# A written-out order of four graph layers: rooms granted by "can every older graph still finish" in place of fixed reserves

## Chip, cores, metric

One core of a Trainium2 chip runs the whole program. The metric is device time in microseconds (us), lower is better. The kernel is launched once; everything it computes is in float32.

## What is computed

32 independent graphs, each with 512 nodes of 256 features `x` and a dense 512 x 512 adjacency `adj`. Every graph goes through four layers, one after the other, and each layer ends in a layer norm over the 256 features:

```python
# layer 0: aggregate with self loop, two dense layers (256 -> 512 -> 256)
x = LN(x + relu(((1 + eps) * x + adj @ x) @ W1 + b1) @ W2 + b2)
# layer 1: dense 256 -> 256, aggregate, leaky relu
x = LN(x + prelu(adj @ (x @ W.T + b), alpha))
# layer 2: norm, aggregate, two dense layers added, relu
h = LN(x) * gamma + beta
x = LN(x + x + relu((adj @ h) @ W_rel + b_rel + h @ W_root))
# layer 3: aggregate, dense 256 -> 1024, RMS norm, silu, dense 1024 -> 256
h = silu(RMS((eps * x + adj @ x) @ W1 + b1) * w)
x = LN(x + h @ W2 + b2)
```

Inside one graph nearly everything hangs on the step before it. Between graphs nothing does.

## The kernel before, in words

**The work of one graph.** All matrix products use a seven-product scheme (`seven`, L651) on half-size blocks: products m1 to m7 go to three PSUM banks that are opened one after the other, and between the products ScalarE or VectorE takes sums out of the banks. A product of `aggregate` (L767) is two matmuls with 256 columns. VectorE makes the sums and differences of blocks that the scheme needs, ScalarE most of the norms' totals, GpSimd the powers of -1/2, SyncE issues all DMAs.

**Buffers.** Three pools (L525 to L527) hold everything that comes and goes: 8 PSUM banks (`banks`), 36 SBUF rooms of 1024 floats per partition (`rooms`; half a room can be given), and 11 small ones (`smalls`). A graph's inputs take three rooms (`load_x` one, `Adjacency` two), and `FLIGHT = 5` (L499) lets at most five graphs hold buffers at once.

**The order.** The kernel does not leave the order to the program text. `do` and `move` (L279, L308) only record operations (`Op`), each with its graph, its possible engines, assumed durations and the operations that must come first. After all 32 graphs are recorded, `best` (L348) runs `order` (L354) once for each tuple of `RULES` and issues the operations in the order of the best one. This takes place when the program is built and costs the chip nothing. What reaches the chip is a fixed order for each engine's queue, and a fixed buffer for each operand.

`order` plays the program through. It gives every operation a `rank`: `graph * period + need`, where `need` (L324) is twice (`pace`) the TensorE work of its graph that lies ahead of it, minus what stands between; the last three graphs (`LATE`) lie only `last` apart. One graph's ranks run over about 142 units, `period` is 42 (the order of the kernel before comes from the tuple 42, 2, 10), so between three and four graphs are interleaved. At each step it takes, among the operations that can start at the earliest moment on an engine, the one of lowest rank. An operation that no TensorE work of its graph waits for (the last norm, the output) has a `need` of about 1000 and so comes last.

An operation that opens a buffer can be taken only if `rooms_free` (L380) allows it. There the change works. Before it, each pool has fixed reserves, `spare`, by the age of the graph (0 for the oldest graph that is not finished, 1 for the next, and so on): a bank is given to the oldest graph if one is free and to a younger one if two are free (0, 1, 1); a room needs 0, 2, 4, 4 further free rooms at ages 0, 1, 2, 3 and up; a small one 0, 2, 4.

```python
                    n += pool.spare[min(op.graph - oldest, len(pool.spare) - 1)]
                    if n >= len(whole):
                        return None
```

The instructions issued for the graphs are the same under any order: the same matmuls, vector, scalar and DMA operations, except that a few copies may go to another engine, and short filler writes (`pause`, L1197) are put in where VectorE has to wait for GpSimd.

Of the kernel before, what the change touches and what calls it, by code (L numbers as in the profile page):

```python
# [14 lines left out]
P = 128  # L15
# [52 lines left out]
ISSUE, ADVANCE, AFTER, LANES = dict(sync=0.45, within=0.66, gpsimd=1.5), 1.5, 0.8, 8  # L68


def wire_time(kbytes):
    return kbytes / 385
# [19 lines left out]

RULES = [(42, 2, 10, 0.5), (42, 2, 16, 0.5)]


class Pool:

    def __init__(self, tiles, grain, spare, psum):
        self.tiles, self.grain, self.spare, self.psum = tiles, grain, spare, psum
        self.clear()

    def clear(self):
# [30 lines left out]
class Room:  # L137
# [2 lines left out]

    def __init__(self, pool, whole=True):
        self.pool, self.whole = pool, whole
        self.uses = 0
        self.clear()

# [75 lines left out]
class Plan:  # L221
# [102 lines left out]
    def needs(self, pace, near):  # L324
# [20 lines left out]
            for op, t, b in zip(self.ops, need, between)  # L345
        ]

    def best(self):  # L348


        rule = min(RULES, key=lambda rule: self.order(*rule)[0])
        return self.order(*rule)[1]

    def order(self, period, pace, last, near):  # L354

        final = max(op.graph for op in self.ops) - LATE
        rank = [
            (min(op.graph, final) * period + max(op.graph - final, 0) * last + need, i)
            for i, (op, need) in enumerate(zip(self.ops, self.needs(pace, near)))
        ]  # L360
        behind = [op.behind for op in self.ops]
        ready = [dict.fromkeys(op.ways, 0.0) for op in self.ops]
        left = {}
        for op in self.ops:
            left[op.graph] = left.get(op.graph, 0) + 1
            for r in op.rooms:
                r.clear()
                r.pool.clear()
        free = dict.fromkeys(("tensor", "vector", "scalar", "gpsimd", "sync"), 0.0)
        oldest, wire, lanes = 0, 0.0, [0.0] * LANES  # L370
        port = dict.fromkeys(free, 0.0)
        powers = {i for i, op in enumerate(self.ops) if op.port and "gpsimd" in op.ways}
        can_start = {i for i, n in enumerate(behind) if not n}
        done = []
        while can_start:
            while oldest in left and not left[oldest]:
                oldest += 1
            room_at = {}

            def rooms_free(op):  # L380

                first = [r for r in op.rooms if r.index is None]
                if not first:
                    return 0.0
                if op.graph - oldest >= self.flight:
                    return None
                at, taken = 0.0, {}
                for r in first:
                    pool = r.pool
                    if pool not in room_at:  # L390
                        room_at[pool] = pool.free()
                    whole, halves = room_at[pool]
                    k = taken.get((pool, False), 0)
                    if not r.whole and k < len(halves):
                        taken[pool, False] = k + 1
                        at = max(at, halves[k][0])
                        continue
                    n = taken.get((pool, True), 0)
                    taken[pool, True] = n + 1
                    n += pool.spare[min(op.graph - oldest, len(pool.spare) - 1)]  # L400
                    if n >= len(whole):
                        return None
                    at = max(at, whole[n][0])
                return at

            best = {}
            for i in can_start:
                op = self.ops[i]
                wait = rooms_free(op)
                if wait is None:  # L410
                    continue
                if op.kbytes and "sync" in op.ways:
                    wait = max(wait, lanes[0])
                at = {
                    e: max(free[e], wait, ready[i][e], port[e] if op.port else 0.0) for e in op.ways
                }
                way = min(
                    at, key=lambda e: at[e] + sum(op.ways[e][0]) + YIELD * (op.yields and e == "vector")
                )
                best.setdefault(way, []).append((at[way], rank[i], i))  # L420
            if not best:
                return 1e12, None
            t, engine = min((min(c)[0], e) for e, c in best.items())
            soon = t + (1e-6 if engine == "tensor" else SOON)
            _, t, i = min((r, s, i) for s, r, i in best[engine] if s <= soon)
            op = self.ops[i]
            op.start, op.way = t, engine
            busy, tail = op.ways[engine][0]
            free_before, free[engine] = free[engine], t + busy
            end = t + busy + tail  # L430
            if engine == "vector":
                idle = t - max(free_before, ready[i][engine])
                op.pause = idle if op.port and t == port[engine] else 0.0
                if op.port:
                    port["gpsimd"] = end
                if any(n in powers for n, _ in op.then):
                    port["vector"] = t + busy + PORT
            if op.kbytes:
                wire = max(wire, t + ADVANCE) + wire_time(op.kbytes)
                end = wire + op.late + AFTER  # L440
                if engine == "sync":
                    lanes = [*lanes[1:], end]
            for r in op.rooms:
                if r.index is None:
                    r.pool.take(r)
                r.left -= 1
                r.until = max(r.until, end + 0.1)
            left[op.graph] -= 1
            for n, result in op.then:
                behind[n] -= 1  # L450
                for e in ready[n]:
                    if e != engine or e != "tensor" and result:
                        ready[n][e] = max(ready[n][e], end + HAND[e])
                if not behind[n]:
                    can_start.add(n)
            can_start.remove(i)
            done.append(op)
        return max(op.start for op in done), done


@with_exitstack
def tile_gnn_stack(ctx: ExitStack, tc: tile.TileContext, a: dict, out: bass.AP):
# [26 lines left out]
    B, N, D = a["x"].shape  # L489
    NC = N // P  # L490
# [8 lines left out]
    FLIGHT, ROOMS, SMALL = 5, 36, 11  # L499

    const = ctx.enter_context(tc.tile_pool(name="const", bufs=1))
    work = ctx.enter_context(tc.tile_pool(name="work", bufs=1))
    psum = ctx.enter_context(tc.tile_pool(name="psum", bufs=1, space=bass.MemoryType.PSUM))
# [12 lines left out]

        return plan.graph in (0, B - 1)

    def pool(kind, name, n, size, grain, spare):
        return Pool(  # L520
            [kind.tile([P, size], F32, tag=f"{name}{i}", name=f"{name}{i}") for i in range(n)],
            grain, spare, kind is psum,
        )

    banks = pool(psum, "ps", 8, N, N, (0, 1, 1))  # L525
    rooms = pool(work, "room", ROOMS, NC * D, P, (0, 2, 4, 4))
    smalls = pool(work, "few", SMALL, 64, 4, (0, 2, 4))  # L527


    def vector(method, n, *args, **kw):  # L530
# [51 lines left out]
    def room(*shape):  # L582
        return Part(Room(rooms)).shaped(*shape)
# [16 lines left out]
    class Wide:  # L600


        def __init__(self, n):
            self.n = n
            self.rooms = [room(2, N) for _ in range(n // 2)]
# [630 lines left out]
```

## Time and profile before

| what | value |
|---|---|
| median of 3 runs | 2318.81 us (2318.75 to 2318.9) |
| span of the profiled execution, first to last instruction | 2317.5 us |
| instructions | 41158, of them 14002 matmul records |
| VectorE, ScalarE, GpSimd busy | 2120.0 us (91%), 1642.6 us (71%), 256.9 us (11%) |
| DMA | 122.83 MB, mean 53 GB/s |
| granted TensorE clock | 0.999 |

The profiled execution's span lies 1.3 us under the median of the runs, which also hold what lies around the span. Nearly all records stand on one line, L298, because every operation is issued by one helper; so groups are told apart by the names of their tiles: `ps` is a bank, `room` a room, `few` a small one, `A` and `L_gnn_W` are weights. A float32 matmul stands in the trace as two records.

Besides the profile's own views, the kernel's recorded operations can be laid beside the trace: every engine runs its instructions in the order in which they were issued, and the counts agree exactly (6989 matmuls at two records and 24 transposes at one make 14002; 5343 vector operations, 161 on GpSimd, 1005 DMAs). This tells to which graph a record belongs, and which buffers are held when. Read so, graph 0 has matmuls from 9.2 to 205.1 us and is done at 261.6 us; graph 3 starts at 42.7 us, graph 4 at 96.9; graph 10 has matmuls from 636.7 to 909.0 us; graph 31, the last, from 2157.6 to 2308.6 us.

### The profile page before, as it was taken

The numbers are of one execution on the slowest core, as the hardware profiler recorded it, in microseconds if no ns is written. First come the engines' busy times: TensorE is split into PE (matmuls) and PEld (weight loads), VectorE is DVE, ScalarE is ACT, GpSimd is POOL, SyncE is SP. The second block draws the span as 40 slices with busy tenths as digits, with TensorE's granted clock in tenths as the row PEclk, the third lists the DMA queues.
The fourth block names the chain that finished last, engine by engine and source line by source line (L and its number), as shares of the span: only waits on it lengthen the run. The fifth ranks groups of instructions, "written<-read, shape, count | busy, mean of one in ns | idle before, by whom it ended". The sixth has DMA issues, their size and how long they took to land.

```text
span 2317.5 us, 41158 instructions
## 1 busy us (share of the span) xinstructions
PE 2295.5 (99%) x14002; PEld 2089.9 (90%) x14002; DVE 2120.0 (91%) x5428; ACT 1642.6 (71%) x4444; POOL 256.9 (11%) x167
## 2 busy tenths in 40 slices
PE   9999999999999999999999999999999999999998
PEld 7889899999999999999999999999999999998988
DVE  8989999999899999999999999989999899989897
ACT  4676677776776776777767776767677677676776
POOL 0000001101101101011011111010110101101110
PEclk9999999999999999999999999999999999999999
DMA  7001222112221122211222211222112222201101
GB/s 241 21 18 19 62 58 60 24 55 62 58 60 28 54 59 65 55 43 41 56 65 57 60 25 56 61 58 59 38 46 58 65 55 52 78 13 24 55 15 42
DMA packets 223746, 122.83 MB, mean 53 GB/s; under 512 B 142896, under 2 KB 194352, under 8 KB 223536
## 3 DMA queue, kind: packets, MB, share of 16 engines
q1 hardware_dynamic: 223536, 120.20, 19.1%
q8 instruction: 111, 1.82, 0.3%
q14 instruction: 99, 0.81, 0.1%
HBM read 78.92 MB, written 24.97 MB: 45 GB/s over the span
## 4 chain that ended last, share of the span: by engine, by line
PE 89%; DVE 7%; ACT 2%; DMA 1%; issue 1%; SPq 0%; POOL 0%; ACTq 0%; DVEq 0%
PE ps L298 89%; DVE room L298 6%; ACT room L298 1%; ACT scrap L298 1%; DVE few L298 1%; DMA room<-in_x_dram 1%; DMA L_gnn_W<-in_L_gnn_W_dram 0%; DMA room<-in_adj_dram 0%; DMA L_gnn_b<-in_L_gnn_b_dram 0%; DMA diagonal<-room 0%; SPq L316 0%; ACT L298 0%; DVE A L298 0%; DVE L_gnn_W_root L298 0%; POOL few L298 0%
## 5 line engine op out<-in xcount | busy, mean ns | idle before, releaser
L298 PE MATMUL ps<-room,room 128*128 128x256 f32 x3584 | 930.9, 381 | 5.7 <-DVE room L298 3.2
L298 DVE TENSOR_TENSOR room<-room,room 128x512 f32<-128x512 f32 (+1 forms) x1360 | 773.0, 590 | 5.4 <-ACT room L298 2.8
L298 DVE TENSOR_TENSOR room<-ps,room 128x256 f32<-128x256 f32 (+1 forms) x1344 | 605.6, 469 | 143.7 <-PE ps L298 136.4
L298 PEld LDWEIGHTS ps<-room,room 128*128 128x128 f32 x3584 | 617.3, 191 | 70.3 <-DVE room L298 7.1
L298 PE MATMUL ps<-L_gnn_W,room 128*128 128x128 f32 (+1 forms) x3584 | 544.3, 290 | 1.9 <-DVE room L298 1.0
L298 PEld LDWEIGHTS ps<-L_gnn_W,room 128*128 128x128 f32 x3584 | 505.6, 191 | 33.7 <-ACT room L298 1.9
L298 PEld LDWEIGHTS ps<-A,room 128*128 128x128 f32 x3072 | 460.5, 191 | 47.3 <-DVE room L298 14.1
L298 PE MATMUL ps<-A,room 128*128 128x128 f32 x3072 | 486.9, 276 | 0.9 <-DVE room L298 0.7
L298 POOL TENSOR_TENSOR few<-few,mhalf 128x4 f32<-128x4 f32 (+2 forms) x161 | 256.2, 1598 | 2054.5 <-DVE few L298 1883.1
L298 ACT ACTIVATE room<-room,few 128x256 f32<-128x256 f32 x627 | 335.0, 596 | 159.9 <-DVE few L298 159.7
L298 PE MATMUL ps<-room,L_gnn_W 128*128 128x256 f32 x1536 | 416.4, 380 | 0.6 <-DVE room L298 0.5
L298 ACT ACTIVATE room<-ps,L_gnn_b_c 128x256 f32<-128x256 f32 x768 | 311.0, 476 | 122.3 <-PE ps L298 117.9
L298 DVE TENSOR_TENSOR room<-room 128x256 f32<-128x256 f32 (+1 forms) x640 | 308.7, 492 | 13.9 <-ACT room L298 8.2
L298 PE MATMUL ps<-room,A 128*128 128x256 f32 x1152 | 320.0, 380 | 1.1 <-ACT room L298 0.8
L298 ACT ACTIVATE room<-room 128x1024 f32<-128x1024 f32 (+2 forms) x260 | 240.8, 939 | 87.3 <-DVE room L298 84.4
L298 PEld LDWEIGHTS ps<-room,L_gnn_W 128*128 128x128 f32 x1536 | 274.5, 191 | 30.1 <-DVE room L298 1.9
L298 ACT ACTIVATE room<-ps 128x256 f32<-128x256 f32 (+1 forms) x513 | 180.1, 373 | 153.3 <-PE ps L298 153.1
L298 ACT ACTIVATE scrap<-room,few 128x256 f32<-128x256 f32 x504 | 250.7, 499 | 39.0 <-DVE few L298 38.3
L298 ACT ACTIVATE scrap<-room 128x256 f32<-128x256 f32 x504 | 206.7, 411 | 88.3 <-DVE room L298 79.8
L298 PEld LDWEIGHTS ps<-room,A 128*128 128x128 f32 x1152 | 202.8, 191 | 22.8 <-ACT room L298 2.0
L298 ACT ACTIVATE room<-room,L_gnn_rms_weight_c 128x512 f32<-128x512 f32 x256 | 173.2, 712 | 13.1 <-DVE room L298 11.0
L298 DVE TENSOR_TENSOR room<-room,loop 128x256 f32<-128x256 f32 x256 | 101.1, 411 | 2.9 <-DMA diagonal<-room 1.8
(57 smaller groups left out, 1110.6 us busy)
## 6 DMA issues: line engine op xcount, KB each, us to landing
room<-in_adj_dram SPq DMA_DIRECT2D x128, 256.0 KB, 5.0
room<-in_x_dram SPq DMA_DIRECT2D x31, 512.0 KB, 5.9
out_dram<-room SPq DMA_DIRECT2D x31, 512.0 KB, 3.2
room<-room SPq DMA_DIRECT2D x480, 32.0 KB, 2.0
diagonal<-room SPq DMA_DIRECT2D x62, 128.0 KB, 1.8
room<-in_adj_dram SPq DMA_DIRECT2D x124, 64.0 KB, 1.9
room<-diagonal SPq DMA_DIRECT2D x62, 128.0 KB, 2.2
room<-line SPq DMA_DIRECT2D x30, 256.0 KB, 3.3
```

The costliest lines, as they stand in the source:

```text
L298: getattr(getattr(self.nc, engine), method)(to, *(put(x) for x in args), **kw)
```

## The change

Three things, all inside the ordering; the recorded operations are not touched.

- `peaks` gives for each operation, by pool, the most buffers that its graph will hold at once from there on. `safe` walks over the graphs in flight from the oldest: each must be able to get what it still needs (its peak, plus one except for banks, less what it holds) out of what is free and what the graphs before it give back. What is left over is what a younger graph may take. `spare` is gone.
- An operation of a graph that is not the oldest, on another engine than TensorE, which would open a buffer, is passed over while its rank is more than `AHEAD` = 70 above that of the first TensorE operation (by rank) not yet placed. Operations with a `need` of `LAST` = 500 or more are exempt.
- `RULES`, tuples of (period, pace, last, near), has (42, 2, 10), (44, 2, 12) and (46, 2, 10) in place of (42, 2, 10) and (42, 2, 16).

```diff
-RULES = [(42, 2, 10, 0.5), (42, 2, 16, 0.5)]
+RULES = [(42, 2, 10, 0.5), (44, 2, 12, 0.5), (46, 2, 10, 0.5)]
+AHEAD, LAST = 70.0, 500.0
...
+    def peaks(self):
+        first, last = {}, {}
+        for i, op in enumerate(self.ops):
+            for r in op.rooms:
+                first.setdefault(r, i)
+                last[r] = i
+        use, held = [], {}
+        for i, op in enumerate(self.ops):
+            for r in op.rooms:
+                if first[r] == i:
+                    k = r.pool, op.graph
+                    held[k] = held.get(k, 0) + r.size
+            use.append({r.pool: held[r.pool, op.graph] for r in op.rooms})
+            for r in op.rooms:
+                if last[r] == i:
+                    held[r.pool, op.graph] -= r.size
+        most, peaks = {}, [None] * len(self.ops)
+        for i in range(len(self.ops) - 1, -1, -1):
+            g = self.ops[i].graph
+            now = dict(most.get(g, {}))
+            for pool, n in use[i].items():
+                now[pool] = max(now.get(pool, 0), n)
+            most[g] = peaks[i] = now
+        return peaks
...
+            def safe(pool, free):
+                most, slack, older = [free], 1e9, 0.0
+                for g in range(oldest, oldest + self.flight):
+                    if left.get(g):
+                        need = peaks[mine[g][reached.get(g, 0)]].get(pool, 0) + (not pool.psum)
+                        has = held.get((pool, g), 0)
+                        slack = min(slack, free + older - max(need - has, 0))
+                        older += has
+                        most.append(slack)
+                    else:
+                        most.append(most[-1])
+                return most
...
-                    n += pool.spare[min(op.graph - oldest, len(pool.spare) - 1)]
-                    if n >= len(whole):
+                    if n >= min(len(whole), most[max(op.graph - oldest, 0)]):
                         return None
...
+            while ahead < len(tensor) and finished[tensor[ahead][1]]:
+                ahead += 1
+            front = tensor[ahead][0] + AHEAD if ahead < len(tensor) else 1e9
...
+                early = op.graph > oldest and front < rank[i][0] and need[i] < LAST
+                if early and "tensor" not in op.ways and any(r.index is None for r in op.rooms):
+                    continue
...
-    banks = pool(psum, "ps", 8, N, N, (0, 1, 1))
-    rooms = pool(work, "room", ROOMS, NC * D, P, (0, 2, 4, 4))
-    smalls = pool(work, "few", SMALL, 64, 4, (0, 2, 4))
+    banks = pool(psum, "ps", 8, N, N)
+    rooms = pool(work, "room", ROOMS, NC * D, P)
+    smalls = pool(work, "few", SMALL, 64, 4)
```

The rest keeps the books: what each graph holds, how far it has come (`reached`), and which operations are placed (`finished`).

More of the change, by code (lines that the diff above doesn't have):

```diff
@@ L90, with __init__ @@
 LATE = 3
-RULES = [(42, 2, 10, 0.5), (42, 2, 16, 0.5)]
+RULES = [(42, 2, 10, 0.5), (44, 2, 12, 0.5), (46, 2, 10, 0.5)]
+AHEAD, LAST = 70.0, 500.0
 class Pool:
-    def __init__(self, tiles, grain, spare, psum):
-        self.tiles, self.grain, self.spare, self.psum = tiles, grain, spare, psum
+    def __init__(self, tiles, grain, psum):
+        self.tiles, self.grain, self.psum = tiles, grain, psum
         self.clear()
@@ L142, in __init__ @@
         self.pool, self.whole = pool, whole
+        self.size = 1.0 if whole else 0.5
         self.uses = 0
@@ L356, in order @@
         final = max(op.graph for op in self.ops) - LATE
+        need = self.needs(pace, near)
         rank = [
-            (min(op.graph, final) * period + max(op.graph - final, 0) * last + need, i)
-            for i, (op, need) in enumerate(zip(self.ops, self.needs(pace, near)))
+            (min(op.graph, final) * period + max(op.graph - final, 0) * last + n, i)
+            for i, (op, n) in enumerate(zip(self.ops, need))
         ]
+        tensor = sorted(r for r, op in zip(rank, self.ops) if "tensor" in op.ways)
         behind = [op.behind for op in self.ops]
@@ L369, in order @@
         free = dict.fromkeys(("tensor", "vector", "scalar", "gpsimd", "sync"), 0.0)
-        oldest, wire, lanes = 0, 0.0, [0.0] * LANES
+        oldest, ahead, wire, lanes = 0, 0, 0.0, [0.0] * LANES
+        peaks, held, mine, reached = self.peaks(), {}, {}, {}
+        for i, op in enumerate(self.ops):
+            mine.setdefault(op.graph, []).append(i)
+        finished = [False] * len(self.ops)
         port = dict.fromkeys(free, 0.0)
@@ L390, in rooms_free @@
                     if pool not in room_at:
-                        room_at[pool] = pool.free()
-                    whole, halves = room_at[pool]
+                        whole, halves = pool.free()
+                        room_at[pool] = whole, halves, safe(pool, len(whole))
+                    whole, halves, most = room_at[pool]
                     k = taken.get((pool, False), 0)
@@ L443, in order @@
             for r in op.rooms:
+                k = r.pool, op.graph
                 if r.index is None:
                     r.pool.take(r)
+                    held[k] = held.get(k, 0) + r.size
                 r.left -= 1
                 r.until = max(r.until, end + 0.1)
+                if not r.left:
+                    held[k] -= r.size
             left[op.graph] -= 1
@@ L457, in order @@
             done.append(op)
+            finished[i] = True
+            n, my = reached.get(op.graph, 0), mine[op.graph]
+            while n < len(my) - 1 and finished[my[n]]:
+                n += 1
+            reached[op.graph] = n
         return max(op.start for op in done), done
@@ L517, in alone, with pool @@
         return plan.graph in (0, B - 1)
-    def pool(kind, name, n, size, grain, spare):
+    def pool(kind, name, n, size, grain):
         return Pool(
             [kind.tile([P, size], F32, tag=f"{name}{i}", name=f"{name}{i}") for i in range(n)],
-            grain, spare, kind is psum,
+            grain, kind is psum,
         )
-    banks = pool(psum, "ps", 8, N, N, (0, 1, 1))
-    rooms = pool(work, "room", ROOMS, NC * D, P, (0, 2, 4, 4))
-    smalls = pool(work, "few", SMALL, 64, 4, (0, 2, 4))
+    banks = pool(psum, "ps", 8, N, N)
+    rooms = pool(work, "room", ROOMS, NC * D, P)
+    smalls = pool(work, "few", SMALL, 64, 4)
     def vector(method, n, *args, **kw):
```

## The prediction

> **What bounds the kernel now.** I read the page's busy times first, then a table of windows, then the groups by shape, then single matmul runs in the timeline, and last the waits of TensorE, by stretches.
>
> ```profile
> PE 2295.5 (99%) x14002; PEld 2089.9 (90%) x14002; DVE 2120.0 (91%) x5428; ACT 1642.6 (71%) x4444; POOL 256.9 (11%) x167
> ```
>
> ```profile
> core 0: us, PE busy (x) PEld busy (x) DVE busy (x) ACT busy (x) POOL busy (x), PEclk, DMA share, GB/s
> 0.00:20.00 20.00, 15.40 (x62) 12.78 (x63) 14.82 (x47) 5.48 (x12) 0.70 (x6) 1.00 0.87 281
> 20.00:120.00 100.00, 96.53 (x537) 83.56 (x537) 96.71 (x266) 62.37 (x175) 6.31 (x5) 1.00 0.33 98
> 120.00:300.00 180.00, 177.41 (x1084) 160.57 (x1083) 164.71 (x422) 124.07 (x328) 17.16 (x12) 1.00 0.13 31
> 300.00:1900.00 1600.00, 1600.00 (x9775) 1461.28 (x9774) 1467.59 (x3727) 1157.32 (x3146) 185.18 (x112) 1.00 0.20 54
> 1900.00:2100.00 200.00, 198.42 (x1198) 180.22 (x1198) 183.42 (x484) 140.91 (x397) 20.09 (x14) 1.00 0.17 45
> 2100.00:2300.00 200.00, 199.27 (x1282) 183.47 (x1282) 186.39 (x460) 139.83 (x353) 24.04 (x15) 1.00 0.09 26
> 2300.00:2318.00 18.00, 8.44 (x74) 8.06 (x72) 6.41 (x28) 12.60 (x40) 3.38 (x4) 0.82 0.30 117
> ```
>
> TensorE (PE) is never idle from 300 to 1900 us; what it loses, it loses in the first 300 us and in the last 400. But "busy" alone can hide a slower stream, so I ask how fast matmuls follow each other when nothing holds them:
>
> ```profile
> 2272.38 1.03 PE L298 MATMUL ps<-room,A 128*128 128x256 f32 x4
> ...
> 2301.76 4.63 PE L298 MATMUL ps<-A,room 128*128 128x128 f32 x40
> ```
>
> ```profile
> L298 PE MATMUL ps<-room,room 128*128 128x256 f32 x3584 | 930.9, 381 | 5.7 <-DVE room L298 3.2 <-DMA room<-in_x_dram 2.5
> ...
> L298 PE MATMUL ps<-A,room 128*128 128x128 f32 x3072 | 486.9, 276 | 0.9 <-DVE room L298 0.7
> ```
>
> Forty 128-column records take 4.63 us, of which the last is 0.276 long: 39 steps of 0.1116 us. Four 256-column records take 1.03, the last 0.381: 3 steps of 0.2163. By the groups there are 7192 records of the first kind (3072 + 3072 + 512 + 512 + 16 + 8) and 6810 of the second (3584 + 1536 + 1152 + 512 + 18 + 8): 802.6 + 1473.0 = about 2276 us. The first matmul starts at 1.2 us and the last at 2308.7, so 2307.5 us hold 2276 of full-rate work and about 32 us of lost time (35 with the mean steps, 0.1112 and 0.2163, of undisturbed neighbours). Summed over the starts of neighbouring matmuls with those means, the 35 lie so: 5.5 before 20 us, 10.7 from 20 to 200, 1.5 to 300, 10 spread over 300 to 1900 in gaps of about 0.1 us, 7.5 after 1900. Behind the last matmul stand 8.8 us of norm and output of graph 31.
>
> Who is late in the head and in the middle, by the waits of TensorE and its weight loads:
>
> ```profile
> PE ps L298 <- DVE room L298: 4.3, 9, 1.5
> PE ps L298 <- DMA room<-in_x_dram: 2.3, 1, 2.3
> PE ps L298 <- ACT room L298: 1.5, 3, 0.7
> ...
> PE ps L298 <- DMA L_gnn_ln_beta_c<-in_L_gnn_ln_beta_dram: 1.1, 1, 1.1
> ```
>
> ```profile
> PEld ps L298 <- DVE room L298: 11.4, 44, 0.3
> PEld ps L298 <- issue: 4.3, 23, 0.3
> ```
>
> The first four are from 0 to 320 us, the last two from 320 to 1900. In the head a result of VectorE ends most waits, and VectorE is 97% busy from 20 to 120 us: there graph 0 is alone at the front, its steps hang on each other, and younger graphs only fill. In the middle no wait exceeds 0.3 us.
>
> **What the Trainium skill says.** "Perfetto Trace Analysis", section "Identifying the Most-Contended Engine", warns that matmul busy share is no measure of headroom and recommends that of LDWEIGHTS; this trace agrees that the 99% needs a second look: the step of 0.1116 us between records of 0.276 us gives it, and the 90% of the weight loads is reached at full rate. The same page, "Optimization Strategy", says that a gap repeating on the engine that should be saturated can mean that there isn't enough SBUF or PSUM for the next tile; from 300 to 1900 us no such gap is here, so more freedom with rooms and banks has nothing to cure there. The page's "Optimizing Tensor Performance" wants independent groups to rotate through PSUM banks so that an evacuation overlaps the next group's matmuls; how many banks a younger graph may rotate through is what the change regulates.
>
> **The change part by part.** The instructions stay, so the floor of 2276 us stays, and so do 1.2 us before, 8.8 behind, and nearly all of the 5.5 before 20 us (the first loads, 2.3 and 1.1 us, stand in the waits; the rest is ahead of any choice between graphs). What the change can win is at most 10.7 + 1.5 + 7.5 = 20 us in head and tail; the 10 us of the middle are too fine for it.
>
> *Rooms and banks in the middle.* I took the order of the kernel before, operation for operation, and applied the new rule's formula at each opening of a buffer: how often would it have said no? From 300 to 1900 us: never, in any pool. Where was the old reserve tight? Over the whole run 265 of 1033 bank openings and 145 of 1469 room openings stood at the old limit. So in the middle the new rule only loosens, on an engine without a gap. The loosening is free but worth 0 us; half of all matmuls there already had their operands 5 us ahead of their start, a quarter less than 2.3. Price between -1 and +2 us, since another order shifts the 0.1 us gaps; I take 0.
>
> *Banks in the head and tail.* Here the rule tightens. An older graph that still has products ahead reserves three banks even while it holds none. Of the bank openings of before, 22 would be refused between 0 and 300 us, 27 between 1900 and 2300. A refused opening moves a fill product of a younger graph (four records, 4 x 0.2163 = 0.87 us of TensorE) to later. If another product is at hand it costs nothing; if none, up to one of the visible waits on VectorE or ScalarE, 5.8 us in 12 waits from 0 to 320 us, 0.48 each. At most 49 x 0.48 = 24 us; below nothing at the other end: the oldest graph, which sets the head's pace, finds a bank at once, and could recover part of those 5.8 us. I take +2 for stalls and -3 for the earlier front: -1.
>
> *Rooms in the head.* Five openings between 113 and 127 us (graphs 1 and 3) would be refused; some minus, some plus, 0.
>
> *Held back.* With period 42, the order of before breaks the new limit of 70 just six times: the openings of the loads of graph 3 (issued at 28.9, 31.0, 33.7 us) and graph 4 (38.1, 41.8, 42.6). No VectorE or ScalarE operation breaks it, so VectorE's load of the head is not relieved. The six wait until the front reaches rank 46 and 88, which before it does at about 50 and 103 us. A load lands in 5 to 6 us. Graph 3 has 0.9 us of matmuls between 40 and 50 us and next to none until 90, graph 4 has 0.9 between 90 and 100 and then none until 200. So at most 1.8 us of fill are lost; in turn SyncE's queue and the DMA engines are freed from 29 to 43 us, where weights of layers 1 and 3 and the restored diagonals go through the same queue: at most the 0.5 + 0.7 us lost at 30.6 and 37.8 us come back. I take +0.5. In the middle a new graph's loads start when the graph five before it is done, at front ranks that allow them at once or some 10 us later, well ahead of use: 0.
>
> *RULES.* The tuple chosen before, (42, 2, 10), stays on offer; two others are added and one goes. A wider period means less interleaving. `best` takes another one only if it plans a shorter end, and what it can plan shorter is head and tail. The last graphs then fit into each other better: of the 7.5 us lost from 1900 on I take 2, between 0 and 4.
>
> Sum: 0 - 1 + 0 + 0.5 - 2 = -2.5 us. On the profiled execution 2317.5 - 2.5 = 2315.0; the median stands 1.3 above the span: 2316.3 us.
>
> **The rivals.** 0.2% of 2318.81 is 4.6 us, about what separates a change from no change here.
>
> 1. *About the same* (chance 0.42): the sum above, with its bounds from -4.6 to +4.6. For it: the middle never refuses. Time 2316.3.
> 2. *Clearly faster* (0.30): the reserve for the oldest graph and the better tail halve what is lost after 20 us outside the middle: (10.7 + 1.5 + 7.5) / 2 = 9.9, less the 1.8 us of lost fill: -8, 2311 us. For it: 72 of the openings by the youngest graphs alone stood at the old bank limit, so the old fill pressed on the old graphs. Against: VectorE is 97% full in the head and gets no relief.
> 3. *Slower* (0.28): three banks lie reserved for an old graph that is in its norm and can't use them, so five are left for all others; TensorE runs dry in the head, and with four graphs abreast also in the tail. Each of the 49 refused openings costs 0.25 us on average: +12 us, 2331. It decides from 4.6 / 49 = 0.09 us each. If the order in the middle also shifts so that the reserve bites there, this grows by some 0.3 us for each of about 22 graphs: +7. Against: such refusals are rare in the old order.
> 4. *The change does nothing* (within rival 1): the order comes out nearly as before, the time within 1 us.
>
> **How the numbers follow.** The likeliest is 1, so 2316.3. The range takes in rival 2 with half again its gain and rival 3 up to nearly its price: 2307 to 2329. The likeliest case's own range is 2314.2 to 2323.4. Chances: faster by over 0.2% 0.30, within 0.42, slower 0.28.
>
> **What would show it.** After the change, PE busy from 300 to 1900 us must stay at 1600 of 1600 (else rival 3 reaches the middle). The loads of graphs 3 and 4 must come after 45 and 85 us. The idle of PE from 20 to 300 us, 6.1 us by the windows, and from 1900 to 2300, 2.3 us, must change by little; if they halve it is rival 2, if waits on banks' evacuation (a PE wait on VectorE or ScalarE rooms) grow there it is rival 3. The matmul count must be 14002 and the tail behind the last matmul about 8.8 us. I am wrong if the middle loses or if the span's end moves by more than the head and the tail can give.

## The result, and the profile after

The changed kernel takes 2326.37 us (median of 5 runs, 2325.61 to 2328.35), the kernel before 2318.9 (2318.75 to 2319.18). The ratio is 1.0031, 95% interval 1.0019 to 1.0042: slower by 0.3%, about 7.5 us. The profiled execution has a span of 2323.8 us against 2317.5. Its matmul count is the same, 14002, and of the three tuples the plan took (42, 2, 10) again, so the edit of `RULES` did nothing. In the plan itself the two orders end alike, with the last operation at 2285.8 us in both: what was lost lies where the chip departs from the plan.

The same windows as those of the kernel before (first and last left out; columns: length, then busy time and records of PE, its weight loads, VectorE, ScalarE, GpSimd, then clock, DMA share, GB/s):

```profile
20.00:120.00 100.00, 95.49 (x525) 82.33 (x524) 94.63 (x262) 62.96 (x179) 6.32 (x5) 1.00 0.34 98
120.00:300.00 180.00, 178.67 (x1104) 162.99 (x1103) 171.20 (x437) 127.25 (x336) 18.12 (x13) 1.00 0.16 42
300.00:1900.00 1600.00, 1595.92 (x9740) 1460.59 (x9739) 1476.26 (x3700) 1136.87 (x3126) 166.95 (x111) 1.00 0.20 52
1900.00:2100.00 200.00, 198.90 (x1200) 181.46 (x1199) 181.30 (x466) 140.76 (x389) 18.64 (x13) 1.00 0.17 43
2100.00:2300.00 200.00, 197.36 (x1246) 179.93 (x1245) 183.16 (x457) 138.51 (x356) 23.19 (x14) 1.00 0.09 26
```

From 300 to 1900 us PE was busy for 1600 of 1600 us; now it is 1595.92. That was the first sign named in the prediction as one that would prove it wrong. The waits of PE and of its weight loads from 320 to 1900 us (total, times, longest):

```profile
PE ps L303 <- DVE room L303: 2.9, 11, 0.3
```

```profile
PEld ps L303 <- DVE room L303: 12.7, 23, 0.7
PEld ps L303 <- issue: 4.2, 22, 0.2
```

Before, PE had no wait at all in this stretch and its weight loads 44 on VectorE of at most 0.3 us. Now there are 23 of up to 0.7 us, about one for each graph that finishes in these 1580 us: a bubble that comes back with every graph.

Lost time, summed over the starts of neighbouring matmuls as in the prediction (step less 0.1112 or 0.2163 us), shows where the 6.3 us between the two spans lie. Here and below the head is 20 to 320 us, the middle 320 to 1900, the tail from 1900 to the last matmul. "Bank waits" are those gaps in the middle in which the operands had long been there, and the last reader of the bank that the matmul opens had just ended; they come from laying the recorded operations beside the trace. Spacing is the mean time between the last matmuls of successive graphs, graphs 5 to 21.

| kernel | head | middle | tail | bank waits | spacing |
|---|---|---|---|---|---|
| before | 12.4 | 9.5 | 7.5 | none | 71.18 |
| after | 11.6 | 15.5 | 9.7 | 7.2 in 23 | 71.46 |

The head is 0.8 us better, the tail 2.2 worse, and the middle 6.0 worse. Before 20 us and behind the last matmul 0.5 and 0.6 us are gained.

One of those waits, in the changed kernel, from 1035 to 1039 us:

```profile
1035.81 0.68 DVE L303 TENSOR_TENSOR room<-room,L_gnn_b 128x512 f32<-128x512 f32 x1
...
1036.41 0.68 DVE L303 TENSOR_TENSOR room<-room,room 128x512 f32<-128x512 f32 x1
...
1037.01 1.76 DVE L303 TENSOR_TENSOR room<-ps,room 128x512 f32<-128x512 f32 x3
...
1038.08 0.30 PEld L303 LDWEIGHTS ps<-room,L_gnn_W 128*128 128x128 f32 x2 [0.44 <-DVE room L303]
1038.08 0.70 PE L303 MATMUL ps<-room,L_gnn_W 128*128 128x256 f32 x2
```

VectorE runs without a gap. The three operations of the 1.76 us group stand under the first one's shape; the second of them takes graph 12's last sum out of a bank (its evacuation) and ends at 1038.02; graph 13's product opens that bank at 1038.08. Its operands had been ready since 1029.67. In the plan there are 0.37 us between the two. VectorE has spent them, since it is late: the next lines show how, a few microseconds earlier.

```profile
1030.59 0.41 DVE L303 TENSOR_TENSOR room<-room,room 128x256 f32<-128x256 f32 x1
1031.02 0.17 DVE L303 TENSOR_TENSOR few<-few 32x16 f32<-32x16 f32 x1
1031.22 0.43 DVE L303 TENSOR_TENSOR room<-room,room 128x256 f32<-128x256 f32 x1
1031.56 0.67 DVE L303 TENSOR_SCALAR few<-few 32x4 f32<-32x4 f32 x4
1032.25 0.43 DVE L303 TENSOR_TENSOR room<-room,loop 128x256 f32<-128x256 f32 x1
```

The four small operations that start at 1031.56 hold VectorE for 0.69 us, until 1032.25; the plan has 4 x 0.064 = 0.26. The small add before takes 0.20 in place of 0.077. Laid beside the plan, VectorE is 0.16 us behind TensorE at 1030.59 and 0.82 us at 1032.25; the whole rise lies in the small add, the four small operations, and about 0.1 us before the add. It stays at 0.82 to 0.85 until 1037.01. The plan has 0.3 us of idle time before the evacuation, which the delay uses up; what is left of it, 0.53 us, is more than the 0.37 that the plan has between evacuation and opening.

In the plan of the kernel before, no bank in the middle is reopened less than 0.7 us after its evacuation; in that of the changed kernel 46 are at under 0.4 us ("tight" below). The old rule "two free banks for a younger graph" was not only a reserve for the oldest graph. It also made a younger graph wait until the second bank was free and then take the one that had been free longest, and so kept a distance in time.

### The profile page after: what moved, and what is told of

It reads as the page before. It is cut to its first block, busy times and chain, and to the rows that moved or that the text cites. A ratio compares the mean times of both kernels' runs of the same rounds, so it can differ in the third digit from the quotient of the medians.

```text
span 2323.8 us, 41098 instructions
## 1 busy us (share of the span) xinstructions
PE 2298.7 (99%) x14002; PEld 2096.1 (90%) x14002; DVE 2134.7 (92%) x5411; ACT 1627.2 (70%) x4438; POOL 238.5 (10%) x167
## 4 chain that ended last, share of the span: by engine, by line
PE 68%; DVE 28%; issue 2%; ACT 1%; DMA 0%; SPq 0%; DVEq 0%; ACTq 0%
PE ps L303 68%; DVE room L303 25%; DVE few L303 2%; ACT room L303 1%; ACT scrap L303 0%; DMA room<-in_adj_dram 0%; DVE A L303 0%; DMA diagonal<-room 0%; DVE pause L1267 0%; DVE L_gnn_W L303 0%; SPq L321 0%; DVEq L303 0%; ACT L303 0%; DVE L_gnn_W_root L303 0%; DVE L_gnn_W_rel L303 0%
## 5 line engine op out<-in xcount | busy, mean ns | idle before, releaser
L303 DVE TENSOR_TENSOR room<-room,room 128x512 f32<-128x512 f32 (+1 forms) x1360 | 774.8, 593 | 12.4 <-ACT room L303 5.9
L303 PE MATMUL ps<-L_gnn_W,room 128*128 128x128 f32 (+1 forms) x3584 | 550.2, 290 | 2.0 <-DVE room L303 1.3
L303 PEld LDWEIGHTS ps<-L_gnn_W,room 128*128 128x128 f32 x3584 | 512.6, 191 | 35.3 <-DVE room L303 2.1
L303 PE MATMUL ps<-A,room 128*128 128x128 f32 x3072 | 481.1, 275 | 2.0 <-DVE room L303 2.0
L303 POOL TENSOR_TENSOR few<-few,mhalf 128x4 f32<-128x4 f32 (+2 forms) x161 | 237.8, 1482 | 2079.6 <-DVE few L303 1966.5
L303 ACT ACTIVATE room<-room,few 128x256 f32<-128x256 f32 x621 | 329.9, 591 | 152.3 <-DVE few L303 149.5
L303 PE MATMUL ps<-room,L_gnn_W 128*128 128x256 f32 x1536 | 422.8, 382 | 5.2 <-DVE room L303 4.7
L303 PE MATMUL ps<-room,A 128*128 128x256 f32 x1152 | 324.7, 381 | 1.2 <-ACT room L303 0.6
L303 PEld LDWEIGHTS ps<-room,L_gnn_W 128*128 128x128 f32 x1536 | 268.5, 191 | 42.8 <-DVE room L303 17.4
L303 DVE TENSOR_TENSOR room<-room,loop 128x256 f32<-128x256 f32 x256 | 106.4, 419 | 6.9 <-PE ps L303 4.6
```

The lines of the kernel that those rows point to most:

```text
L303: getattr(getattr(self.nc, engine), method)(to, *(put(x) for x in args), **kw)
```

## The experiments

All but runs 8, 10 and 11 go with the tuple that both kernels took, (42, 2, 10). The kernel before was timed again beside each group of runs (medians 2319.48 to 2319.67 us), and the ratios are taken against that. First three runs that part the change, and one that tests the explanation in its narrow form.

**1. The old rule for banks in the changed kernel.**

```diff
-                    if n >= min(len(whole), most[max(op.graph - oldest, 0)]):
+                    limit = most[max(op.graph - oldest, 0)]
+                    if pool.psum:
+                        limit = len(whole)
+                        n += op.graph > oldest
+                    if n >= min(len(whole), limit):
```

> The changed kernel with the old rule for banks alone: a younger graph gets a bank only if two are free, as before; rooms and small buffers by the new rule, work far ahead held back, and one tuple, (42, 2, 10), the one that both kernels took. Theory A (the second free bank was a cushion in time: without it a bank is reopened within 0.4 us of its planned evacuation, 46 times in the middle, and TensorE waits for VectorE once per graph, about 0.3 us): the wait per graph goes, the spacing of the outputs from 300 to 1900 us falls from 71.46 back to about 71.18 us per graph, PE busy there is 1600 of 1600, time 2317 to 2321. Rival B (the room rule, or holding work back, makes VectorE late): the spacing stays at 71.4 or more, time 2324 to 2329.

Measured: 2317.36 us, ratio to before 0.9991 (0.9983 to 0.9999), spacing 71.14, middle 8.1 us lost. The window from 320 to 1900 us (length, PE busy, records, clock, DMA share, GB/s), first of the changed kernel and then of this one:

```profile
320.00:1900.00 1580.00, 1575.96 (x9635) 1.00 0.20 52
```

```profile
320.00:1900.00 1580.00, 1579.98 (x9675) 1.00 0.20 53
```

Theory A holds: the bank rule, given the rest of the change, costs 15.5 - 8.1 = 7.4 us in the middle and 9.7 - 4.7 = 5.0 in the tail, and gives back 14.9 - 11.6 = 3.3 in the head, 9.1 in all; the medians differ by 9.0.

**2. Nothing held back.** `AHEAD = 1e9`.

> The changed kernel with nothing held back (AHEAD without end); rooms and banks by the new rule; one tuple, (42, 2, 10). Theory A: the spacing in the middle stays at about 71.46 us per graph with one wait of TensorE on VectorE in each; head and tail change, so the time is 2325 to 2335. Rival B2 (holding back makes VectorE late in the middle): the spacing falls to 71.2, time below 2321.

Measured: 2331.52 us, ratio 1.0053 (1.004 to 1.0065); spacing 71.46, the middle as in the changed kernel to 0.2 us. Holding back has no part in the loss of the middle. It even helps: without it the head loses 17.3 us, with it 11.6. The windows from 20 to 320 us, changed kernel first, show the same in PE's busy time:

```profile
20.00:320.00 300.00, 294.12 (x1733) 1.00 0.22 61
```

```profile
20.00:320.00 300.00, 289.61 (x1702) 1.00 0.22 60
```

**3. The kernel before without a reserve of banks.**

```diff
-    banks = pool(psum, "ps", 8, N, N, (0, 1, 1))
+    banks = pool(psum, "ps", 8, N, N, (0, 0, 0))
```

> The kernel before with one edit of weight: the reserve of banks is gone, (0, 0, 0) for (0, 1, 1); rooms, small buffers and the rest as before; one tuple, (42, 2, 10), the one that it took. Theory A: this alone brings the waits on banks, the spacing of the outputs in the middle rises from 71.18 to 71.4 to 71.6 us per graph, which is 5 to 10 us in all; head and tail come on top, 2324 to 2338. Rival B: the spacing stays at 71.2 and the time moves only by head and tail, within 2316 to 2323.

Measured: 2332.13 us, ratio 1.0055 (1.0042 to 1.0068). The total fits theory A, but for the wrong reason. The middle loses 11.2 us, 1.7 more than before and not 6; the spacing is 71.28, most graphs at 71.13; and no wait on a bank is among the gaps. Of the 12.7 us, 8.1 lie in the head and 2.8 in the tail. Yet this plan has the same 46 tight openings, with the same planned distances of 0.37 and 0.15 us between an evacuation and the reopening by the graph after it. On the chip those distances are 0.46 and 0.24 here, and 0.05 in the changed kernel. Tight banks alone cost nothing. So theory A in its first form fell. The second form, A2: a tight bank costs where VectorE is late at that moment.

The changed kernel holds a control of its own. Of its 46 tight openings 23 are by the next graph, at a planned 0.37 or 0.15 us; VectorE is 0.53 us late there, and these are the 23 waits, of 0.20 and 0.43 us. The other 23 are by an older graph, at a planned 0.36 or 0.10 us; there VectorE is 0.05 to 0.09 us ahead of the plan, the distances come out at 0.42 and 0.19, and no matmul waits on the bank.

**4. A bank counts as free 0.5 us after its last reader in the plan, not 0.1.**

```diff
-                r.until = max(r.until, end + 0.1)
+                r.until = max(r.until, end + (0.5 if r.pool.psum else 0.1))
```

> The changed kernel, all new rules kept, but the plan counts a bank as free 0.5 us after its last reader instead of 0.1 us, with the tuple (42, 2, 10). Theory A in its narrow form (it is the missing time, not the number of banks in use): though the last free bank is still given away, the spacing in the middle falls to 71.2 to 71.3 us per graph and the time to 2316 to 2322. Rival C (it is the number: with all eight banks in use an older graph waits for one, whatever the margin): spacing stays at 71.4 or more, 2324 or more.

Measured: 2342.17 us, ratio 1.0102 (1.0086 to 1.0117), spacing 72.05. The narrow form's figures missed. Rival C's came out (71.4 or more, 2324 or more), but not its mechanism: no wait on a bank is left in the middle, as the narrow form says. The order has another flaw: VectorE now waits for the adjacency of new graphs, nearly once per graph, and TensorE waits for VectorE's sums. VectorE's waits from 300 to 1900 us:

```profile
DVE room L303 <- PE ps L303: 74.5, 122, 1.2
DVE room L303 <- DMA room<-in_adj_dram: 20.9, 23, 1.7
```

The same view of the changed kernel has no wait for a load. This run says nothing on the price of the distance; why its plan brought the loads so late was not followed up.

A2 asks what makes VectorE late. For its lag, take for each VectorE operation the start on the chip less the start in the plan, and subtract the same difference of the TensorE operation issued last. In the changed kernel 3% of VectorE's operations lag by 0.83 us or more; in the kernel before that value is 0.40. Runs 5 to 7 fill in the combinations of the three parts.

**5. Rooms and small buffers by the old reserves, the rest of the change kept.**

```diff
-                    if n >= min(len(whole), most[max(op.graph - oldest, 0)]):
+                    limit = most[max(op.graph - oldest, 0)]
+                    if not pool.psum:
+                        spare = (0, 2, 4, 4) if len(pool.tiles) > 20 else (0, 2, 4)
+                        limit = len(whole)
+                        n += spare[min(op.graph - oldest, len(spare) - 1)]
+                    if n >= min(len(whole), limit):
```

> The changed kernel with rooms and small buffers by the old reserves; banks by the new rule, work held back, tuple (42, 2, 10). Its order has the same tight openings of banks as the changed kernel (46 in the middle under 0.4 us after the planned evacuation). Theory A2, as it stands after the first runs: a tight opening costs only where VectorE is late against the plan at that moment, and it is the new room rule that bunches VectorE's work so. Then the tight openings cost nothing here: 71.1 to 71.25 us per graph in the middle, time 2316 to 2322. Rival A1: the tight openings suffice, or holding back makes VectorE late: 71.4 or more, 2323 to 2330.

Measured: 2321.1 us, ratio 1.0007 (0.9999 to 1.0015); middle 10.4 us, spacing 71.24, no wait on a bank, VectorE's lag 0.54. The same evacuation of graph 12, at the same place, in this kernel's timeline:

```profile
1035.88 0.69 DVE L303 TENSOR_TENSOR room<-ps,room 128x512 f32<-128x512 f32 x1 [1.04 <-PE ps L303]
...
1037.11 0.42 DVE L303 TENSOR_TENSOR room<-ps,room 128x256 f32<-128x256 f32 x1 [0.55 <-PE ps L303]
...
1038.00 0.59 PE L303 MATMUL ps<-room,L_gnn_W 128*128 128x256 f32 x2
```

VectorE has gaps here (the times in brackets), takes the bank out at 1037.11 as soon as the matmul is through, and the bank opens at 1038.00 with 0.46 us to spare. The rival, that tight openings suffice, is out.

**6. Only the room rule.** Banks by the old reserve as in run 1, `AHEAD = 1e9`.

> Rooms and small buffers by the new rule, banks by the old reserve, nothing held back, tuple (42, 2, 10). Theory A2: VectorE is late by 0.8 to 1.1 us in places, as in the changed kernel, but the second free bank covers it: 71.1 to 71.25 us per graph in the middle. Without holding back the head is some 4 to 6 us worse than with it, so 2319 to 2325. Rival: the room rule alone costs in the middle: 71.4 or more, 2324 to 2331.

Measured: 2319.01 us, ratio 0.9998 (0.999 to 1.0006); middle 8.3, spacing 71.14, with VectorE's lag at 1.10 us. Late VectorE alone costs next to nothing: in this plan no bank is reopened less than 1.0 us after its evacuation, and only where a lag of 1.09 meets a planned 1.05 are there 12 waits of 0.09 us each.

**7. Only the holding back, in the kernel before.**

> The kernel before with nothing but the holding back of work far ahead added, tuple (42, 2, 10). Theory A2: the middle stays at 71.18 us per graph. If holding back helps the head by itself, as the pair with and without it at the new rules suggests (16.6 against 22.5 us lost up to 320 us), the time is 2312 to 2318. Rival D: it helps only together with the new rules, and alone takes fill from TensorE in the head: 2320 to 2328.

Measured: 2323.71 us, ratio 1.0019 (1.0012 to 1.0026); middle 9.5, tail 7.5, as before. All of it is in the head, 17.0 against 12.4. Rival D holds: alone it takes away fill, and only with the new rules it is worth having.

**8. Run 1 with another tuple.** `RULES = [(43, 2, 8, 0.5)]`, picked because its planned end is early and no bank in the middle is planned to reopen within 1 us.

> As the first run (banks by the old reserve, rooms by the new rule, work held back), with the tuple (43, 2, 8). In its order every bank in the middle is opened at least 1 us after its planned evacuation. Theory A2: the middle at 71.1 us per graph or a little less, head and tail a few us better than with (42, 2, 10): 2311 to 2316, faster than both kernels. Rival: the tuple matters as much as the rules, and the middle comes out at 71.2 or more: 2317 to 2322.

Measured: 2315.15 us, ratio 0.9982 (0.9974 to 0.999), faster than both kernels, through head (9.5) and tail (6.9). But the middle is not what theory A2 said: 10.4 us lost at a spacing of 71.22, which is the rival's, and the bank waits are back, 7.9 us in 23, 0.34 each. VectorE's lag at these banks is 1.39 us, the planned distance 1.11: the difference, 0.28, is again about what is waited. It made plain that the distance is only the cover, and that the lag is the thing to mend.

**9. The plan's prices for small operations mended.** The adds of `column_sums` and the four of `by_token` get the steps that the changed kernel's trace shows; all three rules of the change stay.

```diff
-            add(few[0:Q], few[0:Q], few[q * Q : (q + 1) * Q])
+            way = "vector", "tensor_add", (0.2, 0.085), (few[0:Q], few[q * Q : (q + 1) * Q]), {}
+            plan.do(few[0:Q], way)
...
-            ts(o[q * Q : (q + 1) * Q], sums[:, q :: P // Q], *ops)
+            way = "vector", "tensor_scalar", (0.168, 0.085), (sums[:, q :: P // Q], s1, s2), kw
+            plan.do(o[q * Q : (q + 1) * Q], way)
```

> The changed kernel, all its rules kept, tuple (42, 2, 10), with one thing mended in the plan: the small VectorE operations on 32 partitions (the adds of column_sums and the four of by_token) are planned at 0.2 and 0.168 us, the steps that the changed kernel's trace shows, instead of 0.077 and 0.064. Theory A2 (tight bank times late VectorE): VectorE's lag behind the plan falls from 0.83 to under 0.4 us, and the tight openings (46 in the middle under 0.4 us, as before) cost nothing: 71.1 to 71.25 us per graph instead of 71.46. Head and tail come out differently, so the total is not the test; 2325 to 2340. Rival A1 (the tight openings cost by themselves): 71.4 or more.

Measured: 2338.39 us, ratio 1.0081 (1.0067 to 1.0095). In the middle VectorE's lag is 0.38 us and no bank is waited for, though 46 are tight, at planned distances of 0.37 and 0.31 us that come out as 0.46 and 0.40. The middle loses 11.8 us with a spacing of 71.32, less than the changed kernel and a little over what was expected: short waits of the weight loads for ScalarE, 5.4 us in 32, have come in. The time is lost in the tail, 23.9 us, with this tuple; one wait of TensorE there, for ScalarE, is 12.1 us long, and the plan has its last operation late too, at 2308.2 us.

**10 and 11. Mended prices with the tuple (45, 2, 12),** picked for its early planned end (last operation at 2283.4 us); once with banks by the old reserve, once by the new rule.

> Banks by the old reserve, rooms by the new rule, work held back, the small VectorE operations priced as measured, tuple (45, 2, 12). Theory A2: VectorE on time and a cushion of banks: 71.1 us per graph in the middle without waits on banks, 2306 to 2313, faster than all others. Rival: VectorE is late for another reason and waits stay at 0.3 us per graph: 2314 or more.

> The same as the run before with banks by the new rule, so that it is the change with its prices mended and another tuple. The two differ by the bank rule alone. Theory A2: with VectorE on time the bank rule costs under 2 us in the middle, and the two are within 4 us of each other. Rival A1: the bank rule costs 6 us or more in the middle here too, 71.4 us per graph.

Measured: 2302.33 us (2301.44 to 2302.49), ratio 0.9925 (0.9912 to 0.9937), with the old bank rule; 2305.39 us (2304.82 to 2307.85), ratio 0.9942 (0.9929 to 0.9954), with the new one. The first is faster than its expected range, 2306 to 2313. Waits of the weight loads on VectorE from 320 to 1900 us are gone in the first, which has no wait of PE or of weight loads to show there; in the second there are

```profile
PEld ps L303 <- DVE room L303: 12.9, 45, 0.6
```

and the middle loses 3.3 against 7.5 us. The pair is within 4 us as A2 said, but the middle's share is 4.2 us and not under 2: 22 bank waits of 0.13 us each are left, at a planned distance of 0.28 us. The mended prices left VectorE with a smaller lag, 0.37 us, not with none. The kernel before in the middle, then the faster of the two, by windows:

```profile
320.00:1900.00 1580.00, 1580.00 (x9667) 1.00 0.20 54
```

```profile
20.00:320.00 300.00, 296.03 (x1764) 267.06 (x1763) 285.90 (x758) 203.49 (x548) 26.23 (x19) 1.00 0.20 53
320.00:1900.00 1580.00, 1580.00 (x9711) 1456.56 (x9710) 1481.93 (x3813) 1141.29 (x3116) 166.86 (x111) 1.00 0.20 54
1900.00:2282.00 382.00, 382.00 (x2400) 353.05 (x2399) 353.64 (x893) 270.94 (x728) 40.97 (x28) 1.00 0.14 36
```

9711 records in 1580 us, where the kernel before has 9667: TensorE gets through more in the same time, at a spacing of 70.91 us per graph, and from 1900 us on it is never idle until the very end.

All runs, in us lost where no other unit is named (lag, in us behind the plan: the value that 3% of VectorE's operations exceed, from 900 to 1114 us):

| kernel | banks | rooms | held back | head | middle | tail | lag | median |
|---|---|---|---|---|---|---|---|---|
| before | old | old | no | 12.4 | 9.5 | 7.5 | 0.40 | 2318.9 |
| run 7 | old | old | yes | 17.0 | 9.5 | 7.5 | 0.40 | 2323.71 |
| run 6 | old | new | no | 18.4 | 8.3 | 4.5 | 1.10 | 2319.01 |
| run 1 | old | new | yes | 14.9 | 8.1 | 4.7 | 1.10 | 2317.36 |
| run 3 | none | old | no | 20.5 | 11.2 | 10.3 | 0.77 | 2332.13 |
| run 5 | new | old | yes | 13.0 | 10.4 | 7.8 | 0.54 | 2321.1 |
| run 2 | new | new | no | 17.3 | 15.3 | 10.0 | 0.83 | 2331.52 |
| after | new | new | yes | 11.6 | 15.5 | 9.7 | 0.83 | 2326.37 |
| run 4 (0.5 us more) | new | new | yes | 13.1 | 28.2 | 9.1 | 0.73 | 2342.17 |
| run 8 (43, 2, 8) | old | new | yes | 9.5 | 10.4 | 6.9 | 1.39 | 2315.15 |
| run 9 (priced) | new | new | yes | 8.6 | 11.8 | 23.9 | 0.38 | 2338.39 |
| run 10 (priced, 45, 2, 12) | old | new | yes | 7.3 | 3.3 | 1.3 | 0.54 | 2302.33 |
| run 11 (priced, 45, 2, 12) | new | new | yes | 7.6 | 7.5 | 1.9 | 0.37 | 2305.39 |

The lag in run 3 is 0.77 and yet it pays nothing at its tight openings: there VectorE is 0.09 us ahead of the plan. It is the lag at the bank that counts, not the highest one.

## Why the prediction was wrong

The forecast was "about the same", 2316.3 us; measured were 2326.37, inside the range that was given and on the other side.

- **The step that failed** is "Rooms and banks in the middle": "The loosening is free but worth 0 us", priced between -1 and +2. It cost 6.0 us, from 9.5 to 15.5. I counted how often the new rule would say no in the old order, found never, and took a looser rule on an engine without a gap as harmless. The count is right, the conclusion from it is not. The question not asked was what the old limit did for the operations that it held: 265 bank openings stood at it, and the limit gave them a distance in time from the evacuation before, 0.7 us or more. The new rule let 46 of them shrink to under 0.4, and 23 of these made TensorE wait for a late VectorE, 7.2 us in all. Half of the matmuls having their operands 5 us ahead was no cover, since operands were not what was late. A bank was.
- The skill's "Perfetto Trace Analysis", section "Optimization Strategy", was read the wrong way round. It says that a repeating gap can mean too little SBUF or PSUM for the next tile. I took the lack of such a gap as a sign that more freedom with banks could do nothing there, also nothing bad. After the change such a gap is there, 0.31 us once per graph. The number of banks is eight as before; what got short is the time between an evacuation and the reopening.
- **"RULES"**, -2 us: the plan took the old tuple, so this was worth nothing, and the tail got 2.2 us worse. Run 1 shows why: with the old banks the tail would have lost 4.7 us, with the new ones it loses 9.7.
- **"Banks in the head and tail"**, -1 us: wrong in the tail, where they cost 5.0 (run 1 against the changed kernel), better than thought in the head, +3.3 us gained. Of the tail's 5.0 us four waits on tight banks make 1.2; whether the rest is the refused openings of the prediction, the runs don't tell.
- **"Held back"**, +0.5 us: right in the middle (run 2 changes nothing there), wrong in size in the head. It depends on what it is combined with: alone it costs 4.6 us (12.4 to 17.0), with the other rules it saves 5.7 (17.3 to 11.6). The 1.8 us of fill that I counted in the old order was too little; the order changes, and the first matmul of graph 3 moves from 42.7 to 94.2 us, that of graph 4 from 96.9 to 208.6.
- **"Rooms in the head"**, 0: alone the room rule costs 6.0 us in the head and gains 3.0 in the tail (run 6).
- Rival 3 had the direction and nearly the price (2331), but named the opposite mechanism: too few banks for the young graphs, in head and tail. It also named the observation that decides, PE busy in the middle under 1600.
- What held: the floor of matmuls, their count, about 8 us behind the last matmul (8.2 in place of 8.8), the loads of graphs 3 and 4 after 45 and 85 us (at 51.5 and 100.9), and that head and tail move by little (-0.8 and +2.2 us). For the head that was luck: in the order before, run 6, run 1, after, the room rule costs 6.0 us there, holding back returns 3.5 and the bank rule 3.3, where I had 0, +0.5 and a part of -1.

What the runs show together is an interaction. In the middle the bank rule costs about 1 us with old rooms (run 5 against run 7), the room rule gains 1.2 us with old banks (run 6 against before), and both together cost 6. One takes the cover away, the other makes VectorE late. That the lateness builds up in the small operations is read from the trace of one graph above. That their prices let it happen is supported by run 9, which differs from the changed kernel in the prices alone and has no wait on a bank in the middle, against 7.2 us; but its order differs in other ways that come of the prices. How much of the 17 us of run 10 is due to the prices and how much to the tuple is open. It was not tried with the old prices and (45, 2, 12) under otherwise equal rules. Why the room rule bunches VectorE's work was not followed further either.

## What to carry to other kernels

A reserve that never seems to refuse anything useful can be a cushion in time: before it is taken away, look at how long the buffers at the limit had been free when they were reused, and how late their last reader can be. If an order is planned ahead, compare its starts with the trace engine by engine; where one engine drifts within each period, mend its price first, and then choose the order anew: with the old tuple the mended prices lost 23.9 us in the tail (run 9), with another 1.3 (run 10). And count not only what a new rule would refuse of the old order, but what it will newly allow.

## What was not expected of the hardware

Small VectorE operations hold the engine much longer in some forms than in others, though their rows look alike. Rows of the changed kernel from 500 to 1782 us (busy, mean ns):

```profile
L303 DVE TENSOR_SCALAR few<-few 128x2 f32<-128x2 f32 x144 | 23.2, 161 | 11.3 <-ACT scrap L303 9.4
L303 DVE TENSOR_TENSOR few<-few 32x16 f32<-32x16 f32 x108 | 17.8, 164 | 2.8
...
L303 DVE TENSOR_SCALAR few<-few 32x4 f32<-32x4 f32 x72 | 11.4, 158 | 0.7
```

All three take about 160 ns by their rows. From start to start, with work waiting behind, a 128x2 `tensor_scalar` takes 0.070 us (84 of them, before a `tensor_sub`), a 32x4 one 0.163 to 0.175 (97, each before another), and a 32x16 `tensor_add` about 0.20 (155 of 192). The Trainium skill's "VectorE: DVE Perf Modes", section "The TRN2 errata", says that operations with SBUF sources pay a fixed extra latency per instruction, which many small tiles pay again and again; here one form pays some 0.1 us that another does not.

Neither the 32 partitions nor the dependence on the operation before explains it. Over the traces of all runs, a 32x16 `tensor_scalar` that stays on the first 32 partitions takes 0.076 us (252). The last of the four 32x4 operations takes 0.175 to 0.194 before operations that do not use its result (392); the first of the four, before such operations, takes 0.071 (24). What the slow ones share, by the kernel's text, is that they join different groups of 32 partitions: the later three of `by_token` read one group and write another, and the adds of `column_sums` take their operands from two. The operation before such a one is drawn in: the first of the four takes 0.16 when the second follows. And such an add takes 0.093 us when the operation behind it reads a bank (437), but 0.198 before a large one that reads rooms alone (1138). Why, these runs don't show.
